# Two-tile groups and a three-stage output in the last layer of a four-layer graph network on one Trainium2 core

## The chip, the cores and the metric

The kernel runs on one core of one Trainium2 chip. The metric is the time of one execution on the device in microseconds (us); of several executions the median counts. TensorE is called PE, VectorE DVE, ScalarE ACT, GpSimd POOL, and SyncE, which here only issues transfers, SP.

## What is computed

Four layers run one after the other on 4096 nodes with 128 features; `adj` is a 4096 x 4096 float32 matrix with few nonzero entries. Each layer adds its result to `x` and normalizes the rows. The change lies in the last layer (L3), and this layer is overlapped with the one before it (L2, attention over the edges):

```python
# L2: attention over the edges of adj (C from per-node scores)
tau = adj_t * jnp.exp(jnp.maximum(0.2 * C, C))
att_weights = tau / jnp.sum(tau, axis=1, keepdims=True)
z = jnp.einsum('mnh,nhf->mhf', adj_t * att_weights, h_prime)
x = _layernorm(x + z.reshape(n, heads * f_out) + bias)
# L3
deg = jnp.clip(jnp.sum(adj, axis=1, keepdims=True), 1.0)
x = _layernorm(x + x @ W_self + (adj @ x / deg) @ W_neigh)
```

## The kernel before

The 4096 rows are 32 tiles of 128 (`NT`), or 8 blocks of 512 (`NB`); `TB` is 4. Layers 0 and 1 are dense products with `adj` and end near 1311 us of the profile. Beside them DVE makes a list of each row's nonzero entries. What follows uses this list (`sparse_layers`, L1405).

**The loop over the tiles** (L1699 to L1724) does layer 2 for tile t, and layer 3 for the tiles before it. The order of PE, DVE, ACT and POOL is the order of the program (L1653); nothing is reordered. In turn:

- POOL issues nine gathers for tile t + 2 (`gathers`, L1491), with a small operation after every second one. The tile `got` has four buffers.
- PE multiplies some *units* of layer 3. A unit is one 128 x 512 float32 product in `layer3_product` (L1597); the profile counts it as two matmuls. `multiply(n)` (L1665) takes n units, and before each one DVE adds finished sums to `acc3` (`add_up`, L1609). With `held=True` nothing is added, and it ends once two sums wait.
- `edges(t)` (L1513) is layer 2's chain for the tile, mostly on DVE: scores, Exp on ACT (L1529), the weighted rows `gw` (L1532), and the sum `here` (L1534). `sums` (L1537) on PE, `divide` (L1544) on DVE and `turn` (L1553), a transpose and the row statistics, follow.
- At the last tile of a *group*, `layer3_rows` (L1560) is put into a queue called `chains`, and three steps of it are taken: a copy on ACT (L1564) with the root for 1/std, the product with W3 on PE (L1573), and the scaling on ACT of `y` (L1577) and `x` (L1583), after which ACT loads Exp's table again (L1584). In the next iteration `begin` (L1673) puts the group's units into the queue `pieces`; so a group's units can start one iteration after its last tile.

The groups are listed in `sizes` (L1696): 1, 1, 2, then six groups of 4, then 2, 1, 1. A group of n tiles has 8 n units; n of them accumulate in one PSUM tile, which DVE then adds to `acc3` in one addition (L1615; the first group is copied by ACT, L1613). The adjacency comes in loads of 1 MB with five buffers (`columns`, L1589), each for 4 / n blocks. The last tile has no units; the output phase takes it in.

Per iteration there are places for 2 + 1 units before `edges`, 4 held ones beside it, 2 held ones after `sums`, and 3 at the end. The last column of `y`, which makes the row sums of `adj`, is set to 1 by a DVE memset after each scaling (L1578). `y` lies in the buffer of `xT`.

**The output phase** (L1729 to L1736) takes the 8 blocks in turn. `layer3_end` (L1617): PE transposes `acc3` back and adds the last tile's share (L1625, L1627); DVE takes 1/deg, and makes the four rows `o` (L1632); ACT squares three of them (L1638), and DVE one (L1640). After the `yield` come the root on ACT (L1643), its reciprocal on DVE (L1644), the scaling on ACT and POOL (L1648, L1650), and SP's store (L1651). The second half of block ib - 1 is issued after the first half of block ib. `o` lies in the tile `rows`, which has room for all 8 blocks.

Of the kernel before, what the change touches and what calls it, by code (L numbers as in the profile page):

```python
# [11 lines left out]
F32 = mybir.dt.float32  # L12
# [4 lines left out]
AF = mybir.ActivationFunctionType  # L17
ALU = mybir.AluOpType
# [3 lines left out]
P = 128  # L22
IB = 512
TB = IB // P
# [19 lines left out]
def adj_resnorm_d4(ctx: ExitStack, tc: tile.TileContext, x_in, xT_in, adj, adjT, w0g, w0gT, a0, w1a, b1a,  # L44
# [7 lines left out]
    nc = tc.nc  # L52
    N, F = x_in.shape
    NT = N // P
    NB = N // IB
# [1349 lines left out]
    def sparse_layers(enter, lists, w, h0T):  # L1405
# [85 lines left out]
        def gathers(t):  # L1491
            if t >= NT:
                return
            got[t] = l2.tile([P, E, F + H], F32, name="got", bufs=4)
            for j in range(E):
                nc.gpsimd.indirect_dma_start(got[t][:, j, :], None, table,  # L1496
                                             bass.IndirectOffsetOnAxis(ap=lists.source[:, t, j:j + 1], axis=0))
                if j % 2:
                    lists.pause()
# [60 lines left out]
        def layer3_rows(t0, n):  # L1560

            s = small.tile([P, n], F32, name="rstd2")
            xb = l2.tile([P, n, P], F32, name="oT")
            nc.scalar.copy(xb, turned.pop(t0))  # L1564
            inverse(s, mv[:, t0:t0 + n, 1])
            yield
            qs = []
            for k0 in range(0, n, 2):
                m = min(2, n - k0)
                q = ps_x.tile([P, m, 2, F], F32, name="px")  # L1570
                qs += [(k0 + k, q[:, k]) for k in range(m)]
                for k in range(m):
                    nc.tensor.matmul(q[:, k].rearrange("p s f -> p (s f)"), xb[:, k0 + k, :],  # L1573
                                     W3.rearrange("p s f -> p (s f)"), start=True, stop=True)
            yield
            for k, q in qs:
                nc.scalar.activation(y[:, t0 + k, :], q[:, 0, :], AF.Copy, scale=s[:, k:k + 1])  # L1577
                nc.vector.memset(y[:, t0 + k, F - 1:F], 1.0)  # L1578
            for k, q in qs:
                if n == 1:  # L1580
                    nc.vector.tensor_scalar_mul(x[:, t0 + k, :], q[:, 1, :], s[:, k:k + 1])
                else:
                    nc.scalar.activation(x[:, t0 + k, :], q[:, 1, :], AF.Copy, scale=s[:, k:k + 1])  # L1583
            nc.scalar.activation(warm, eps, AF.Exp)  # L1584
            yield
# [31 lines left out]
        def layer3_end(t0, n, ib, a):  # L1617


            p = ps_p.tile([P, TB, F], F32, name="pp")  # L1620
            o = rows[:, ib * TB:(ib + 1) * TB, 0:F]
            s = small.tile([P, 2, TB], F32, name="less", bufs=3)
            for k in range(TB):
                at = slice(ib * IB + k * P, ib * IB + (k + 1) * P)
                nc.tensor.matmul(p[:, k, :], acc3[:, at], ident, start=True, stop=False)  # L1625
                for r in range(n):
                    nc.tensor.matmul(p[:, k, :], a[:, r, k * P:(k + 1) * P], y[:, t0 + r, :], start=False, stop=r == n - 1)  # L1627
            r = small.tile([P, TB], F32, name="rdeg")
            nc.vector.tensor_scalar_max(r, p[:, :, F - 1], 1.0)
            nc.vector.reciprocal(r, r)  # L1630
            for k in range(TB):
                nc.vector.scalar_tensor_tensor(o[:, k, 0:F - 1], p[:, k, 0:F - 1], r[:, k:k + 1], x[:, ib * TB + k, 0:F - 1],  # L1632
                                               op0=ALU.mult, op1=ALU.add, accum_out=s[:, 0, k:k + 1])
            nc.vector.tensor_scalar_mul(o[:, :, F - 1], s[:, 0, :], -1.0)
            for k in range(TB):
                junk = l2.tile([P, F], F32, name=f"z{k // 3}")
                if k < 3:
                    nc.scalar.activation(junk, o[:, k, :], AF.Square, accum_out=s[:, 1, k:k + 1])  # L1638
                else:
                    nc.vector.scalar_tensor_tensor(junk, o[:, k, :], 1.0, o[:, k, :], op0=ALU.mult, op1=ALU.mult,  # L1640
                                                   accum_out=s[:, 1, k:k + 1])
            yield
            nc.scalar.activation(s[:, 1, :], s[:, 1, :], AF.Sqrt, bias=eps, scale=1.0 / F)  # L1643
            nc.vector.reciprocal(s[:, 1, :], s[:, 1, :])  # L1644
            for k in range(TB):
                scale = s[:, 1, k:k + 1]
                if k < 2:
                    nc.scalar.activation(o[:, k, :], o[:, k, :], AF.Copy, scale=scale)  # L1648
                else:
                    nc.gpsimd.tensor_scalar(o[:, k, :], o[:, k, :], scale, None, op0=ALU.mult)  # L1650
            nc.sync.dma_start(out[ib * IB:(ib + 1) * IB, :].rearrange("(k p) f -> p k f", p=P), o)  # L1651

        with tc.manual_schedule(engines={mybir.EngineType.PE, mybir.EngineType.DVE, mybir.EngineType.Activation,  # L1653
                                         mybir.EngineType.Pool}):
            chains, pieces = deque(), deque()

            def one(queue, n=1):
                while queue and n:
                    r = next(queue[0], queue)
                    if r is not queue:  # L1660
                        n -= 1
                    else:
                        queue.popleft()

            def multiply(n, held=False):  # L1665
                for _ in range(n):
                    if not held:
                        add_up()
                    elif len(adds) > 1:
                        break  # L1670
                    one(pieces)

            def begin(t0, n):  # L1673
                pieces.append(layer3_product(t0, n))
                return
                yield

            for ib in range(NB):
                p = ps_p.tile([P, IB], F32, name="pp")
                for c in range(NB):  # L1680
                    a = chunk(ld, adjT, ib, c)
                    for k in range(TB):
                        nc.tensor.matmul(p, w[:, c * TB + k, :], a[:, k, :], start=c == 0 and k == 0,  # L1683
                                         stop=c == NB - 1 and k == TB - 1)
                    one(chains)
                end = block_end(ib, p)
                next(end)
                chains.append(end)
            load_spread(0)
            while chains:  # L1690
                one(chains)
            gathers(0)
            gathers(1)
            lists.check()
            targets(0)
            sizes = [1, 1, 2] + [TB] * 6 + [2, 1, 1]  # L1696
            groups = [(sum(sizes[:i]), n) for i, n in enumerate(sizes)]
            of = {t: g for g in groups for t in range(g[0], sum(g))}
            for t in range(NT):  # L1699
                t0, n = of[t]  # L1700
                gathers(t + 2)
                if t % TB == 1:
                    load_spread(t // TB + 1)
                targets(t + 1)
                multiply(2)
                one(chains)
                multiply(1)
                add_up()
                multiply(4, held=True)
                made = edges(t)  # L1710
                add_up()
                if t == t0 + n - 1:
                    nc.scalar.activation(warm, eps, AF.Sqrt)
                so = sums(*made)
                multiply(2, held=True)
                divide(t, so)
                turn(t, t0, n)
                if t == t0 + n - 1:
                    chains.append(layer3_rows(t0, n))
                    if t < NT - 1:  # L1720
                        chains.append(begin(t0, n))
                for _ in range(3):
                    one(chains)
                    multiply(1)  # L1724
            while chains or pieces:
                one(chains)
                multiply(2)
            add_up()
            ends = deque()  # L1729
            late = [columns(NT - 1, 1, ib) for ib in range(0, NB, TB)]  # L1730
            for ib in range(NB):
                ends.append(layer3_end(NT - 1, 1, ib, late[ib // TB][:, ib % TB]))
                next(ends[-1])
                if ib:
                    next(ends.popleft(), None)
            next(ends.popleft(), None)  # L1736

    network(True)
    with tc.If(nc.values_load(flag[0:1, 0:1], min_val=0, max_val=2 * P) != 0):
# [33 lines left out]
```

## Time and profile before

| | us |
|---|---|
| median of 3 runs (1900.08 to 1912.03) | 1908.64 |
| profiled execution, its own time | 1786.93 |
| span of its instructions | 1785.1 |
| first and last gather on POOL start | 1335.57, 1707.81 |
| first matmul of the output phase (L1625) | 1744.59 |
| store instructions of the output phase | 1755.05 to 1775.85 |
| PE, DVE, ACT, POOL busy in the span | 1632.3, 1066.5, 350.9, 435.3 |

All times inside the profile are us from the start of the span. Rows of a timeline give start, duration, engine, line, operation, output and input with their shapes, the count of instructions merged in the row, and in brackets how long the engine was idle before it and what ended this. A group row gives busy time and the mean in ns, then the idle time before the group's instructions. The profiled execution is 6.4% below the median of the runs; the granted clock of TensorE, mean 0.955 over the span, is known for the profiled execution only.

### The profile page before, as it was taken

How to read it: one execution, taken by the hardware profiler on the slowest of the kernel's cores; microseconds unless marked ns; L12 is line 12 of the kernel's file. 1: busy time of each engine (PE TensorE's matmuls, PEld its weight loads, DVE VectorE, ACT ScalarE, POOL GpSimd, SP SyncE). 2: the span in 40 equal slices, each digit the busy share in tenths (PEclk: the TensorE clock that was granted, in tenths of full speed). 3: DMA queues.
4: the chain of work that ended last, by engine and by line, in shares of the span. 5: the costliest groups of instructions: out<-in, count | busy, mean ns of one | idle time of the engine just before them, and what ended most of it. 6: DMA issues, size and time to landing. Idle time of an engine off the chain costs nothing.

```text
span 1785.1 us, 15746 instructions
## 1 busy us (share of the span) xinstructions
PE 1632.3 (91%) x4964; PEld 773.6 (43%) x4968; DVE 1066.5 (60%) x3043; ACT 350.9 (20%) x628; POOL 435.3 (24%) x636
## 2 busy tenths in 40 slices
PE   7999999999999999999999999999965677888794
PEld 3344445544444444444444444444432344444443
DVE  6655447888877876767966421232334655655664
ACT  5865501100000110101000000121222111111123
POOL 0000000000000000000463543000008888888822
PEclk9999999999999999999999999999986788888897
DMA  9987665788888567656878778888874566766682
GB/s 384 373 324 278 247 219 183 247 319 304 294 296 305 212 247 256 249 212 245 291 257 285 273 273 296 300 296 291 296 208 115 195 198 213 238 226 230 219 233 69
DMA packets 89791, 455.04 MB, mean 255 GB/s; under 512 B 15585, under 2 KB 25826, under 8 KB 40674
## 3 DMA queue, kind: packets, MB, share of 16 engines
q1 hardware_dynamic: 68112, 422.93, 66.6%
q0 software_dynamic: 12288, 19.54, 4.6%
q10 hardware_dynamic: 9298, 11.47, 1.9%
q8 instruction: 41, 0.67, 0.1%
q14 instruction: 52, 0.43, 0.1%
HBM read 446.48 MB, written 7.41 MB: 254 GB/s over the span
## 4 chain that ended last, share of the span: by engine, by line
PE 73%; POOL 8%; DVE 8%; DMA 5%; issue 3%; ACT 2%; ACTq 0%; DVEq 0%; SPq 0%; POOLq 0%
PE pacc L687 35%; PE pp L1683 12%; PE pacc L397 11%; POOL got L1496 7%; PE pp L1604 4%; DMA chunk<-in_adjT 2%; DVE here L1534 2%; PE pmm L716 1%; DMA got<-table,source 1%; DVE gw L1532 1%; DMA keep<-in_adjT 1%; PE ptr L397 1%; PE pden L385 1%; PE px L1573 1%; PE ptr L155 1%
## 5 line engine op out<-in xcount | busy, mean ns | idle before, releaser
L1496 POOL DMA_INDIRECT got<-table,source x288 | 276.4, 960 | 307.4 <-issue 304.0
L1386 POOL DMA_INDIRECT value<-in_adjT,where x96 | 99.2, 1034 | 639.3 <-DVE bad L1314 527.2
L1604 PE MATMUL pp<-chunk,xT 128*128 128x512 f32 x496 | 234.6, 619 | 1.3 <-DVE xT L1578 1.0
L687 PE MATMUL pacc<-chunk,v 128*128 128x512 f32 x512 | 225.4, 595 | 0.0
L1683 PE MATMUL pp<-chunk,w 128*128 128x512 f32 x512 | 224.6, 592 | 0.0
L687 PE MATMUL pacc<-chunk,t 128*128 128x512 f32 x512 | 223.5, 592 | 0.0
L687 PE MATMUL pacc<-chunk,x 128*128 128x512 f32 x512 | 222.1, 592 | 0.0
L397 PE MATMUL pacc<-chunk,hw 128*128 128x512 f32 x408 | 186.7, 601 | 0.9 <-DVE hw L439 0.7
L1274 DVE MAX8 top<-chunk 128x8 f32<-128x512 f32 x224 | 144.1, 681 | 59.3 <-DMA chunk<-in_adjT 59.3
L1275 DVE FIND_INDEX8 at<-top,chunk 128x8 uint16<-128x512 f32 x224 | 151.3, 686 | 0.0
L687 PEld LDWEIGHTS pacc<-chunk,v 128*128 128x128 f32 x512 | 95.9, 190 | 117.0 <-issue 117.0
L687 PEld LDWEIGHTS pacc<-chunk,x 128*128 128x128 f32 x512 | 96.2, 190 | 115.8 <-issue 115.8
L687 PEld LDWEIGHTS pacc<-chunk,t 128*128 128x128 f32 x512 | 96.1, 190 | 115.3 <-issue 115.0
L1683 PEld LDWEIGHTS pp<-chunk,w 128*128 128x128 f32 x512 | 95.1, 190 | 109.3 <-issue 108.6
L1604 PEld LDWEIGHTS pp<-chunk,xT 128*128 128x128 f32 x496 | 93.1, 199 | 98.3 <-issue 89.5
L397 PEld LDWEIGHTS pacc<-chunk,hw 128*128 128x128 f32 x408 | 74.1, 190 | 91.0 <-issue 85.9
L328 DVE TENSOR_SCALAR pos<-chunk 128x2048 bf16<-128x2048 f32 x66 | 80.4, 1222 | 44.8 <-DMA chunk<-in_adjT 42.0
L369 ACT ACTIVATE junk<-chunk 128x2048 fp8e4<-128x2048 f32 x51 | 97.4, 1909 | 23.3 <-DMA chunk<-in_adjT 22.6
L1615 DVE TENSOR_TENSOR acc<-pp,acc 128x512 f32<-128x512 f32 x80 | 54.6, 687 | 68.7 <-PE pp L1604 68.5
L1540 PE MATMUL so<-gw,into 128*128 128x132 f32 x192 | 34.5, 325 | 59.4 <-DVE gw L1532 59.4
L1249 POOL IOTA i<- 128x384 int32 (+3 forms) x4 | 1.0, 259 | 331.8 <-PE pden L385 317.7
L1540 PEld LDWEIGHTS so<-gw,into 128*128 128x128 f32 x192 | 29.4, 224 | 76.0 <-issue 42.2
(303 smaller groups left out, 1665.8 us busy)
## 6 DMA issues: line engine op xcount, KB each, us to landing
chunk<-in_adjT SPq DMA_DIRECT2D x386, 1024.0 KB, 4.9
keep<-in_adjT SPq DMA_DIRECT2D x13, 1024.0 KB, 7.8
spread<-spread ACTq DMA_DIRECT2D x16, 384.0 KB, 5.3
got<-table,source POOLq DMA_INDIRECT x288
table<-rows ACTq DMA_DIRECT2D x8, 264.0 KB, 6.5
xT<-in_xT ACTq DMA_DIRECT2D x8, 256.0 KB, 8.0
out<-rows SPq DMA_DIRECT2D x8, 256.0 KB, 2.3
value<-in_adjT,where POOLq DMA_INDIRECT x96
```

Of the source, the lines that this page charges most:

```text
L328: r = nc.vector.tensor_scalar(pos, a, 0.0, None, op0=ALU.is_gt)
L369: nc.scalar.activation(junk, a, AF.Relu, scale=-1.0, accum_out=bad[:, n:n + 1], saturate=False)
L397: in_order(nc.tensor.matmul(p, hw[:, j * TB + k, :], a[:, k, :], start=first and k == 0, stop=last and k == TB - 1))
L687: nc.tensor.matmul(p, stationary(c * TB + k), a[:, k, :], start=n == 0 and k == 0, stop=n == NB - 1 and k == TB - 1)
L1274: nc.vector.max(self.top[:, t, ib, :], row)
L1275: nc.vector.max_index(self.at[:, t, ib, :], self.top[:, t, ib, :], row)
L1386: pin(nc.gpsimd.indirect_dma_start(self.value[:, c * TB + k, j:j + 1], None, flat, bass.IndirectOffsetOnAxis(ap=self.where[:, c * TB + k, ...
L1496: nc.gpsimd.indirect_dma_start(got[t][:, j, :], None, table, bass.IndirectOffsetOnAxis(ap=lists.source[:, t, j:j + 1], axis=0))
L1540: nc.tensor.matmul(so, into[:, j, :], gw[:, j, :], start=j == 0, stop=False)
L1604: nc.tensor.matmul(p, y[:, t0 + k, :], a[:, ib % (TB // n), k, :], start=k == 0, stop=k == n - 1)
L1615: nc.vector.tensor_add(acc3[:, blk], p, acc3[:, blk])
L1683: nc.tensor.matmul(p, w[:, c * TB + k, :], a[:, k, :], start=c == 0 and k == 0, stop=c == NB - 1 and k == TB - 1)
```

## The change

Three edits. The groups of layer 3 become 1, 1, fourteen times 2, 1, 1. The column of ones in `y` is set once, ahead of the loop, and the scaling on ACT writes 127 columns. The output phase's `layer3_end` has three stages: up to DVE's square; ACT's squares and root; reciprocal, scaling and store. Stage three of block ib - 1 is issued between stage one and stage two of block ib. `o` becomes a tile of its own with three buffers.

```diff
             for k, q in qs:
-                nc.scalar.activation(y[:, t0 + k, :], q[:, 0, :], AF.Copy, scale=s[:, k:k + 1])
-                nc.vector.memset(y[:, t0 + k, F - 1:F], 1.0)
+                nc.scalar.activation(y[:, t0 + k, 0:F - 1], q[:, 0, 0:F - 1], AF.Copy, scale=s[:, k:k + 1])
...
-            o = rows[:, ib * TB:(ib + 1) * TB, 0:F]
+            o = l2.tile([P, TB, F], F32, name="o", bufs=3)
...
             nc.vector.tensor_scalar_mul(o[:, :, F - 1], s[:, 0, :], -1.0)
-            for k in range(TB):
-                junk = l2.tile([P, F], F32, name=f"z{k // 3}")
-                if k < 3:
-                    nc.scalar.activation(junk, o[:, k, :], AF.Square, accum_out=s[:, 1, k:k + 1])
-                else:
-                    nc.vector.scalar_tensor_tensor(junk, o[:, k, :], 1.0, o[:, k, :], op0=ALU.mult, op1=ALU.mult,
-                                                   accum_out=s[:, 1, k:k + 1])
+            junk = [l2.tile([P, F], F32, name=f"z{k}") for k in range(2)]
+            nc.vector.scalar_tensor_tensor(junk[1], o[:, 3, :], 1.0, o[:, 3, :], op0=ALU.mult, op1=ALU.mult,
+                                           accum_out=s[:, 1, 3:4])
             yield
+            for k in range(3):
+                nc.scalar.activation(junk[0], o[:, k, :], AF.Square, accum_out=s[:, 1, k:k + 1])
             nc.scalar.activation(s[:, 1, :], s[:, 1, :], AF.Sqrt, bias=eps, scale=1.0 / F)
+            yield
             nc.vector.reciprocal(s[:, 1, :], s[:, 1, :])
...
             gathers(1)
+            nc.vector.memset(y[:, :, F - 1], 1.0)
             lists.check()
             targets(0)
-            sizes = [1, 1, 2] + [TB] * 6 + [2, 1, 1]
+            sizes = [1, 1] + [2] * 14 + [1, 1]
...
-            for ib in range(NB):
-                ends.append(layer3_end(NT - 1, 1, ib, late[ib // TB][:, ib % TB]))
-                next(ends[-1])
+            for ib in range(NB + 1):
+                if ib < NB:
+                    ends.append(layer3_end(NT - 1, 1, ib, late[ib // TB][:, ib % TB]))
+                    next(ends[-1])
                 if ib:
                     next(ends.popleft(), None)
-            next(ends.popleft(), None)
+                if ib < NB:
+                    next(ends[-1])
```

## Prediction

> **What bounds the kernel now.** I read the page first. Its section 5 shows POOL's gathers, 288 of 0.96 us with short gaps:
>
> ```profile
> L1496 POOL DMA_INDIRECT got<-table,source x288 | 276.4, 960 | 307.4 <-issue 304.0
> ```
>
> They start at 1335.57 and 1707.81; POOL's timeline has no gap over 0.31 us between, so a tile takes 372.2 / 287 x 9 = 11.67 us of POOL. Is that the pace of the loop? DVE's timeline has L1526, which reads the gathered rows, at tiles 20, 24, 28 and 31:
>
> ```profile
> 1589.32 0.17 DVE L1526 TENSOR_TENSOR score<-got,near 128x24 f32<-128x24 f32 x1
> 1637.45 0.18 DVE L1526 TENSOR_TENSOR score<-got,near 128x24 f32<-128x24 f32 x1
> 1685.60 0.17 DVE L1526 TENSOR_TENSOR score<-got,near 128x24 f32<-128x24 f32 x1
> 1725.84 0.17 DVE L1526 TENSOR_TENSOR score<-got,near 128x24 f32<-128x24 f32 x1
> ```
>
> Four tiles take 48.14 us, POOL needs 46.7: the loop itself is slower, and falls behind. Tile 31's gathers were issued by 1708.8 and read 17 us later. So the loop's own chain counts.
>
> The early group of tiles 2 and 3 already has the new size, and shows what its chain costs. PE's timeline over tiles 4 and 5, which multiply its 16 units:
>
> ```profile
> 1394.45 2.08 PE L1573 MATMUL px<-W,oT 128*128 128x256 f32 x4 [0.46 <-ACT oT L1564]
> 1396.32 0.28 PE L1511 MATMUL u<-dst,spread 128*128 128x13 bf16 x3
> 1397.11 5.76 PE L1604 MATMUL pp<-chunk,xT 128*128 128x512 f32 x8 [0.52 <-DVE xT L1578]
> 1402.71 0.84 PE L1540 MATMUL so<-gw,into 128*128 128x132 f32 x6
> 1403.38 0.41 PE L1541 MATMUL so<-here,ident 128*128 128x132 f32 x2
> 1403.63 1.88 PE L1604 MATMUL pp<-chunk,xT 128*128 128x512 f32 x4
> 1405.35 0.29 PE L1557 MATMUL px<-ident,x 128*128 128x128 f32 x1
> 1405.47 2.74 PE L1604 MATMUL pp<-chunk,xT 128*128 128x512 f32 x6
> 1408.05 0.22 PE L1511 MATMUL u<-dst,spread 128*128 128x13 bf16 x3
> 1408.12 6.25 PE L1604 MATMUL pp<-chunk,xT 128*128 128x512 f32 x14
> ```
>
> Two matmuls are a unit: 4 + 2 + 3 + 7 = 16, then none are left. And DVE's L1532 of tiles 3, 4, 5:
>
> ```profile
> 1388.51 1.35 DVE L1532 TENSOR_TENSOR gw<-got,u 128x1152 f32<-128x1152 f32 x1
> 1400.03 1.35 DVE L1532 TENSOR_TENSOR gw<-got,u 128x1152 f32<-128x1152 f32 x1
> 1413.46 1.35 DVE L1532 TENSOR_TENSOR gw<-got,u 128x1152 f32<-128x1152 f32 x1
> ```
>
> Group end to next tile 11.52 us; from there to the second tile 13.43 us.
>
> In the output phase (1744.6 to 1775.5) the DVE groups show the wait to be removed, and the line of stores how long one takes to land:
>
> ```profile
> L1644 DVE RECIPROCAL less<-less 128x4 f32<-128x4 f32 x8 | 1.4, 178 | 9.2 <-ACT less L1643 9.2
> DMA to landing us min/median/max: 2.3/2.3/3.9
> ```
>
> [...] a unit is 0.86 us at 1408 and about 1.7 us at 1397, after an idle PE. [...] The trace has the 1.28 us, but the next ACT operation starts 0.01 us later, so I take 1.28. [...]
>
> **Part 1: groups of two.** Bytes, loads (64), matmuls of units stay. DVE gets 17 x 8 - 8 = 128 additions for 80, 48 x 0.69 = 33 us more. Most of it fits into DVE's waits for PE at L1615 (60.1 us). On the path lies this:
>
> - Group end to next tile: divide, transpose, copy, W3, scaling, table load, Exp, with no units left to cover it: 11.52 us, plus what the now two additions ahead of L1547 cost. L1547 started 4.11 us after L1532 at tile 3 (no addition), 4.33 us at tile 5 (two): + 0.22. At tile 5 the transpose already ran at the slow clock (0.48 us), so I take W3 slow too, as at tile 3 (2.08 us). Sum 11.74.
> - Next tile to second tile: as measured, 13.43.
> - A pair: 25.17 us. Two tiles of a group of four take 24.07. A group of four pays the uncovered passage once for four tiles, the new groups twice.
>
> From L1532 of tile 4 (1400.03, unchanged, since the groups before are the same) to that of tile 30 are 13 pairs: 1400.03 + 13 x 25.17 = 1727.24; before, 1714.31. + 12.93.
>
> Tile 30 to 31: before 12.82. By position in the queue, DVE's last addition ahead of `edges(31)` now follows the third unit instead of the second: one unit, + 0.86.
>
> Backlog after tile 31's W3: before, the timeline has 26 matmuls, 13 units (11.32 us). Counting the places (9 units in a first, 7 in a second tile of a pair) tile 30 starts with 16 units, leaves 7, tile 31 begins with 2, gets 8 more, takes 10 by its end; 3 remain, and 2 come after W3: 5. Gain 8 x 0.86 = 6.9.
>
> Start of the output phase: 1744.59 + 12.93 + 0.86 - 6.9 = 1751.5, **+ 6.9**. The lag behind the gathers grows to about 29 us; a `got` buffer would be late only at some 30, so POOL is not held up.
>
> **Part 2: ones.** 31 memsets of 0.06 us go, with waits of 24.9 us for ACT (DVE's waits, 1371 to 1708). I cost this at nothing: after a group end `edges` waits for Exp, which stands behind the table load on ACT (Exp at 1399.30, its scores ready at 1398.33). Were the load not there, the gain would be about 1 us per pair, 14 in all. The new strided memset is not in the trace: between 0.06 (L1578) and 0.7 us (L1615), on a DVE idle for 13.45 us before tile 0.
>
> **Part 3: output.** Before, a block takes 3.23 us between reciprocals, of which DVE waits 0.98 for the root. Moved behind the next block's first half, the reciprocal would find the root done: 3.23 - 0.98 = 2.25 us. The first block gains more: Sqrt's table load (1751.92) now follows the first squares; first reciprocal at 1751.5 instead of 1753.55. Moved with it: scaling, and SP's store, alone in SP's queue. ACT has 3 squares, root, 2 scalings, some 2.2 us per block: it just fits. The last block pays: its squares stand behind the scaling of block 6, + 1.1 us.
>
> The new `o` has three buffers: block ib waits for the store of block ib - 3. Reciprocal to the end of POOL's scaling is 1.47 us (1753.55 to 1755.02), landing 2.3: 3.8; from the first L1632 to the next reciprocal 1.75, with hand-overs 1.85. Two blocks per 5.65 us, so 2.83 each, not 2.25. Reciprocals, in the old time scale: block 0 at 1751.5, then 2, 4, 6 at 1757.2, 1762.9, 1768.55; the last 2.1 later, at 1770.65. Before: 1773.97. **- 3.3**. Without the buffers' limit it would be about - 5.9.
>
> **Sum.** 6.9 - 3.3 = + 3.6 us on the profile's 1786.93. The runs' median is 1.068 times that, of unknown cause; I scale: + 3.9, **1912.5 us**. Some 1% is what a measurement of this kernel can tell from no change.
>
> **Rivals.**
>
> - *W3 runs at the fast clock* after a group end (PE multiplied 7 units just before): 1.03 instead of 2.08 us, a pair 24.12, 13 x 1.05 = 13.7 us less: - 10.1, scaled - 10.8, 1898. Against: the slow transpose at tile 5. Chance 0.14.
> - *The gathers become the bound*: the loop needs no more than POOL, 23.33 us a pair: 13 x 1.84 = 23.9 less, - 20.3, scaled - 21.7, 1887. For: shorter backlogs, no memset waits. Against: tiles 3 to 5. Chance 0.07.
> - *The output doesn't get shorter*: stores land after 3.9 us (the maximum), two blocks per 7.15 us, and block 7 at 1775.3: + 1.3 instead of - 3.3; sum + 8.2, scaled + 8.8, 1917. The change then doesn't do what it says. Chance 0.15.
> - *Slower*: after each group end PE stays slow for longer. At tile 4 it was fast after 7 us from W3's start (1394.45 to about 1401.5), in groups of four after 5.2. [...] + 25.7, scaled + 27.4, 1936. Chance 0.14.
> - The forecast: 0.50, its own range 1906 to 1919.
>
> Range: forecast, third and first rival hold 0.79 and reach from about 1892 to 1922 with the 0.3% by which the runs scatter; I take the upper end to 1932[...]. Faster by over 1% (below 1889.6) is the second rival with the tail of the first, 0.08; slower by over 1% (above 1927.7) most of the fourth, 0.13; within, 0.79.
>
> **What would show it.** L1532 of tiles 4, 6, 8 some 25.2 us apart, W3 at 2.1 us for 4 matmuls, no units between a group end and its W3; L1625 first at 1751; 10 matmuls after tile 31's W3; L1615 128 times; DVE idle ahead of L1632 on a store from block 3 on, blocks 2.8 us apart. Wrong would be a pair near 23.3 or above 26, gathers with gaps, or a wait at L1644.

## The result, and the profile after

The changed kernel takes 1904.05 us (median of 22 runs, 1901.6 to 1906.74), the kernel before 1904.68 us (22 runs, 1888.9 to 1912.28) beside it. The ratio is 1.000, 95% interval 0.9984 to 1.0015. The forecast was 1912.5 us, + 0.2% on the 1908.64 us shown; no difference was measured, and + 0.2% lies just above the interval.

The profiled execution of the kernel after spans 1902.6 us and agrees with its runs. That of the kernel before, 1785.1 us, did not agree with its own. So the two traces differ by 117.5 us where the runs differ by nothing, and no difference between them may be put down to the change before that is cleared up.

Where are the 117.5 us? Up to the first gather both are alike (1335.6 and 1336.7 us). After it, in the groups of the profile after (busy us, mean ns, idle before, what ended most of it):

```profile
L1496 POOL DMA_INDIRECT got<-table,source x288 | 277.5, 964 | 412.3 <-issue 302.8
L1603 PE MATMUL pp<-chunk,xT 128*128 128x512 f32 x496 | 266.7, 681 | 37.7 <-DVE acc L1614 27.3
...
L1614 DVE TENSOR_TENSOR acc<-pp,acc 128x512 f32<-128x512 f32 x128 | 83.5, 684 | 104.5 <-PE pp L1603 59.2
```

The gathers cost what they did (0.96 us each), but POOL now stood idle for 412.3 us instead of 307.4. The additions are 128, as forecast. The units wait for additions (27.3 us), and the additions for units: a circle, so something in it must be late. Two tiles in DVE's timeline, from the L1532 of tile 13, the last of its group, to that of tile 15:

```profile
1590.82 1.35 DVE L1532 TENSOR_TENSOR gw<-got,u 128x1152 f32<-128x1152 f32 x1
...
1601.47 1.35 DVE L1532 TENSOR_TENSOR gw<-got,u 128x1152 f32<-128x1152 f32 x1
...
1613.83 0.69 DVE L1614 TENSOR_TENSOR acc<-pp,acc 128x512 f32<-128x512 f32 x1 [4.29 <-PE pp L1603]
1618.08 1.89 DVE L1614 TENSOR_TENSOR acc<-pp,acc 128x512 f32<-128x512 f32 x3 [3.56 <-PE pp L1603]
...
1621.74 1.35 DVE L1532 TENSOR_TENSOR gw<-got,u 128x1152 f32<-128x1152 f32 x1
```

And PE in the second half of it:

```profile
1609.27 4.44 PE L1603 MATMUL pp<-chunk,xT 128*128 128x512 f32 x6
1613.55 0.22 PE L1511 MATMUL u<-dst,spread 128*128 128x13 bf16 x3
1613.63 2.93 PE L1603 MATMUL pp<-chunk,xT 128*128 128x512 f32 x6
1618.83 3.83 PE L1603 MATMUL pp<-chunk,xT 128*128 128x512 f32 x5 [2.27 <-DVE acc L1614]
```

From group end to the next tile it takes 10.65 us (forecast 11.74), but from there to the second tile 20.27 us (forecast 13.43). In this second part PE's rows say that three units were done by 1613.7 and three more by 1616.6; DVE adds one at 1613.83, and the next only at 1618.08, three in a row. PE in turn has no free PSUM tile until 1618.8. Nothing in the rows occupies DVE between 1614.5 and 1618.1: it waits for a signal of PE.

In the output phase the wait for the root is smaller now (L1642 waits 3.1 us in all, L1644 waited 9.2 before), and a wait for the stores has come. DVE's reciprocals, and the rows' computation where it waits:

```profile
1872.23 0.18 DVE L1642 RECIPROCAL less<-less 128x4 f32<-128x4 f32 x1 [0.58 <-ACT less L1640]
...
1874.65 0.18 DVE L1642 RECIPROCAL less<-less 128x4 f32<-128x4 f32 x1 [0.24 <-ACT less L1640]
...
1876.16 0.35 DVE L1631 SCALAR_TENSOR_TENSOR o<-pp,rdeg,x 128x127 f32<-128x127 f32 x1 [1.06 <-POOL o L1648]
...
1877.79 0.17 DVE L1642 RECIPROCAL less<-less 128x4 f32<-128x4 f32 x1
...
1878.55 0.35 DVE L1631 SCALAR_TENSOR_TENSOR o<-pp,rdeg,x 128x127 f32<-128x127 f32 x1 [0.33 <-DMA out<-o]
...
1880.21 0.18 DVE L1642 RECIPROCAL less<-less 128x4 f32<-128x4 f32 x1
...
1881.68 0.35 DVE L1631 SCALAR_TENSOR_TENSOR o<-pp,rdeg,x 128x127 f32<-128x127 f32 x1 [1.03 <-DMA out<-o]
...
1883.31 0.17 DVE L1642 RECIPROCAL less<-less 128x4 f32<-128x4 f32 x1
```

From block 3 on DVE waits for the store of three blocks ago (the row at 1876.16 names POOL, which had done its scaling before; the two later ones name the store). Two blocks take 5.5 to 5.6 us. From the first matmul of the phase to the end it is 37.1 us, before 40.0 (there the matmul's row starts at 1745.02; the 1744.59 of the table above is its weight load).

### The profile page after: what moved, and what is told of

Its sections match the earlier page's. It is cut to its first block, busy times and chain, and to the rows that moved or that the text cites. A ratio compares the mean times of both kernels' runs of the same rounds, so it can differ in the third digit from the quotient of the medians.

```text
span 1902.6 us, 15801 instructions
## 1 busy us (share of the span) xinstructions
PE 1663.1 (87%) x4964; PEld 773.8 (41%) x4968; DVE 1091.3 (57%) x3066; ACT 372.1 (20%) x664; POOL 436.4 (23%) x636
## 2 busy tenths in 40 slices
DMA packets 95935, 455.04 MB, mean 239 GB/s; under 512 B 15585, under 2 KB 25826, under 8 KB 52962
## 3 DMA queue, kind: packets, MB, share of 16 engines
q1 hardware_dynamic: 74256, 422.93, 63.8%
## 4 chain that ended last, share of the span: by engine, by line
PE 74%; DVE 10%; DMA 5%; issue 4%; another core or an unknown queue 4%; ACT 2%; POOL 1%; DVEq 0%; ACTq 0%; SPq 0%; POOLq 0%
PE pacc L687 33%; PE pp L1681 12%; PE pacc L397 10%; PE pp L1603 8%; DMA chunk<-in_adjT 2%; DVE here L1534 2%; DVE acc L1614 2%; DVE gw L1532 2%; PE pmm L716 1%; PE px L1573 1%; DMA keep<-in_adjT 1%; PE ptr L397 1%; PE ptr L155 1%; PE pden L385 1%
## 5 line engine op out<-in xcount | busy, mean ns | idle before, releaser
L1496 POOL DMA_INDIRECT got<-table,source x288 | 277.5, 964 | 412.3 <-issue 302.8
L1603 PE MATMUL pp<-chunk,xT 128*128 128x512 f32 x496 | 266.7, 681 | 37.7 <-DVE acc L1614 27.3
L1603 PEld LDWEIGHTS pp<-chunk,xT 128*128 128x128 f32 x496 | 101.0, 219 | 154.3 <-issue 99.6
L1614 DVE TENSOR_TENSOR acc<-pp,acc 128x512 f32<-128x512 f32 x128 | 83.5, 684 | 104.5 <-PE pp L1603 59.2
L1557 PE MATMUL px<-ident,x 128*128 128x128 f32 x32 | 11.5, 361 | 75.1 <-issue 35.5
L1529 ACT ACTIVATE score<-score 128x36 f32<-128x36 f32 x32 | 7.4, 231 | 281.0 <-DVE score L1528 281.0
```

What stands on the lines that cost most here:

```text
L1496: nc.gpsimd.indirect_dma_start(got[t][:, j, :], None, table, bass.IndirectOffsetOnAxis(ap=lists.source[:, t, j:j + 1], axis=0))
L1603: nc.tensor.matmul(p, y[:, t0 + k, :], a[:, ib % (TB // n), k, :], start=k == 0, stop=k == n - 1)
L1614: nc.vector.tensor_add(acc3[:, blk], p, acc3[:, blk])
```

## The experiments

All in all eighteen runs, in five sets. The runs of a set are on one chip, and the kernel before runs beside them. Times of a set are compared within it.

### First set: the change in parts (kernel before: 1890.98 us)

**The kernel before, unchanged**, to see a second profile of it.

> The kernel before, unchanged. Theory A (the first profile of it is typical, its 1785.1 us span stands for the runs): a second profile is again near 1785, four tiles of the loop take 48 us, and the 6% between profile and runs stays unexplained. Theory B (the loop over the tiles has waits in the usual run that the first profile did not have; the changed kernel's profile, span 1902.6 against runs of 1904, has them): the second profile is near 1900, the layers up to 1345 us are unchanged, and the loop from the first gather to the last takes about 490 us instead of 372.

Measured: 1889.68 us, ratio 1.000 (0.9983 to 1.0017); profile 1880.0 us. The step from tile 1 to tile 2 is 50.9 us (12.2 in the first profile), the steps at the ends of the groups of four are 16.6 to 21.3 us (13.9), and that from tile 8 to 9 is 29.0 us (12.6). From the first gather to the last it is 436 us; theory B holds, though it had said 490. These waits are in the kernel before too. The first profile showed an execution without them. What are they? The longest, all engines in one timeline, at tile 1:

```profile
1366.68 0.81 PE L1541 MATMUL so<-here,ident 128*128 128x132 f32 x2 [0.86 <-DVE here L1534]
...
1378.85 0.20 POOL L1392 TENSOR_TENSOR idle<-idle 128x1 f32<-128x1 f32 x1
1378.85 0.18 DVE L1547 RECIPROCAL rd<-so 128x4 f32<-128x4 f32 x1 [12.22 <-remote]
...
1379.83 0.45 PE L1557 MATMUL px<-ident,x 128*128 128x128 f32 x1 [9.41 <-DVE x L1549]
...
1384.44 0.38 SPq L1594 DMA_DIRECT2D chunk<-in_adjT  x1
...
1392.15 0.27 ACT L1564 COPY oT<-px 128x128 f32<-128x128 f32 x1 [26.54 <-remote]
```

PE's last matmul into `so` is done at 1367.5 by its row; DVE, which needs only that, starts at 1378.85, 11.4 us later. PE's transpose is done at 1380.3; ACT, which needs only that, starts at 1392.15, 11.9 us later. (The 26.54 us in its row are all of ACT's idle time.) SP's load needs a buffer that PE has read with its fourth unit, whose row ends at 1369.2; the load goes at 1384.44. The same tile in the first profile of before:

```profile
1365.87 0.49 PE L1541 MATMUL so<-here,ident 128*128 128x132 f32 x2 [0.86 <-DVE here L1534]
1366.40 0.18 DVE L1547 RECIPROCAL rd<-so 128x4 f32<-128x4 f32 x1 [0.58 <-PE so L1541]
...
1367.91 0.27 PE L1557 MATMUL px<-ident,x 128*128 128x128 f32 x1
1368.22 0.27 ACT L1564 COPY oT<-px 128x128 f32<-128x128 f32 x1 [3.04 <-PE px L1557]
```

Here DVE and ACT start 0.04 us after the rows' ends, and SP's load 0.03 us after the fourth unit. In other directions nothing is late: in the second profile DVE's result at 1379.68 is taken by PE at 1379.83, DVE's `here` by PE within 0.06 us in 31 of the 32 tiles, and ACT's Exp by DVE after 0.03 us in all of them; the last two hold in the kernel after too. So in this stretch PE's completions reach DVE, ACT and SP 11 to 15 us late, while signals to PE, and from ACT to DVE, are prompt. In the groups after it ACT's copy (L1564) is on time (in the kernel after 0.04 us behind the transpose's row in each of them); there it is DVE that waits (in the kernel after 104.5 us in all at L1614). Whether the matmuls or their signals were late can't be told from the rows. I call both "held" in what follows.

**Groups of two alone** (`sizes` as in the change, all else as before).

> Only the groups of two. Theory A: +6.9 us on the path, scaled +7.4, ratio 1.004. Theory B: the loop waits for something that does not depend on the groups, so 0 within 0.2%; the profile near 1900 with a pair of tiles about 31 us and not 25.2.

Measured: 1904.17 us, ratio 1.0066 (1.0041 to 1.0091): + 12.5 us by the ratio. Theory A said + 7.4; the sign is right, the size nearly double. Of theory B the long pairs came true (30.3 us on average from tile 6 to 28, 30.5 in the kernel after), its "0 within 0.2%" did not.

**The output phase alone** (three stages, `o` with three buffers).

> Only the three-stage output with its three buffers for o. Both theories: the output phase's reciprocals are 2.8 us apart instead of 3.23, in all -3.3 us, scaled -3.5, ratio 0.998. If the buffers bind more (store landing 3.9 us) +1.3 us; if they do not bind -5.9 us.

Measured: 1888.94 us, ratio 0.9988 (0.9968 to 1.0007), a gain too small for the runs' scatter. The trace shows it: first output matmul to the end 38.1 us, and 40.1 in the kernel before, so - 2.0 where - 3.3 was forecast.

**The ones alone** (set once, no memsets).

> Only the column of ones set once. Theory A: 0, as the Exp behind the table load is later anyway. Rival: up to 7 group ends gain 1 us each, -7 us, ratio 0.996.

Measured: 1891.66 us, ratio 1.0009 (0.9994 to 1.0024). Nothing, as forecast.

### Second set: take the gathers away (kernel before: 1893.75 us)

The held stretches all lie where POOL issues gathers. For the kernels before and after, the gathers of the later tiles are left out:

```diff
         def gathers(t):
             if t >= NT:
                 return
-            got[t] = l2.tile([P, E, F + H], F32, name="got", bufs=4)
+            if t >= 4:
+                got[t] = kept[t % 4]
+                return
+            got[t] = kept[t] = l2.tile([P, E, F + H], F32, name="got", bufs=4)
```

> The kernel before, but POOL gathers rows for tiles 0 to 3 only, and the later tiles read those rows again (that part of the computation is left out). Everything else keeps its instructions. Theory A, the gathers in flight hold back the other engines in the usual runs (the loop's steps at a group end are 18 to 23 us there and were 13.9 in the first profile): from tile 4 on four tiles take 48 us or less, group end to next tile about 13.9, and the run is 50 to 80 us shorter, ratio 0.957 to 0.974. The long wait between tiles 1 and 2 (51 us), which lies beside the first gathers, stays. Theory B, the waits come from TensorE, the chunk loads or the engines' own queues: steps stay at 50 to 58 us per four tiles, run within 10 us, ratio 0.995 to 1.0.

> The kernel after with the same part left out: gathers for tiles 0 to 3 only. Theory A: a pair of tiles takes what the prediction's chain said, 11.7 + 13.4 = 25.2 us instead of the 30.4 measured in the kernel after (of which 18.6 to 20.3 lay between the first and the second tile of a pair). Then the chain was right and the gathers made the difference; this kernel is 3 to 8 us slower than the kernel before with few gathers. Theory B: pairs stay near 30 us, with 18 to 20 us from first to second tile.

Measured: 1799.0 us (0.9519, 0.9441 to 0.9597) and 1803.94 us (0.9535, 0.9458 to 0.9613). Theory A holds in both, though the first is 95 us shorter than before where 50 to 80 were expected (some 3 of the 95 are POOL's drain at the very end of the program, 2.2 us instead of 5.5). The rows' transfers and POOL's pauses go with the gathers, so these runs do not tell which of them matters. The kernel before has steps of 13.9, 12.5, 12.6 and 9.0 us in each group of four from tile 7 on, 48.1 us together. The kernel after without its later gathers, DVE's timeline from tile 16, the first of its group, to tile 18:

```profile
1570.62 1.35 DVE L1536 TENSOR_TENSOR gw<-got,u 128x1152 f32<-128x1152 f32 x1
...
1577.97 0.69 DVE L1618 TENSOR_TENSOR acc<-pp,acc 128x512 f32<-128x512 f32 x1 [1.08 <-PE pp L1607]
1579.85 0.69 DVE L1618 TENSOR_TENSOR acc<-pp,acc 128x512 f32<-128x512 f32 x1 [1.19 <-PE pp L1607]
1581.57 0.69 DVE L1618 TENSOR_TENSOR acc<-pp,acc 128x512 f32<-128x512 f32 x1 [1.02 <-PE pp L1607]
...
1584.02 1.35 DVE L1536 TENSOR_TENSOR gw<-got,u 128x1152 f32<-128x1152 f32 x1
...
1595.31 1.35 DVE L1536 TENSOR_TENSOR gw<-got,u 128x1152 f32<-128x1152 f32 x1
```

13.40 us from the first to the second tile, where the prediction's chain had 13.43, and 10.6 to 11.7 us over the group ends (11.29 in the rows). An addition waits 1.0 to 1.2 us for its unit, where it waited 3.6 to 4.3. The chain of instructions is the same; only the gathers are gone.

In both kernels the stretch beside the first 36 gathers stays: 31.8 and 31.5 us from tile 1 to 2.

**A pause behind every gather** in the kernel after, instead of every second (POOL's operation of 0.20 us).

```diff
-                if j % 2:
-                    lists.pause()
+                lists.pause()
```

> The kernel after, with POOL's short pause (0.20 us) behind every gather instead of every second one; nothing is left out. A tile then takes 9 x 1.32 us of POOL or a little more. If an unbroken string of gathers holds back the others and a pause lets them go (one form of theory A), first to second tile falls from 18.6 to 20.3 towards 13.4 us and the run is 20 to 60 us shorter (0.97 to 0.99). If a pause lets nothing go, or the gathers are not the cause (theory B), the steps and the time stay, ratio 0.998 to 1.003.

**The kernel after again**.

> The kernel after, unchanged, for the sum of the parts: groups alone gave 1.0066, output alone 0.9988, ones alone 1.0009, all on one chip. If the parts add up and the chip is like that one: 1.0063, 0.4 to 0.8% slower than before. If the three parts together hide one another's cost, or the kernel before is as slow as in the first comparison: 1.000, as measured first.

Measured: 1876.17 us with the pauses (0.9939, 0.9913 to 0.9965), 1911.03 us without (1.011, 1.0028 to 1.0193): 35 us less for adding work to POOL. The interval of the second, with four runs, takes in the forecast of 1.0063 and leaves out that of 1.000. First to second tile takes 14.1 to 20.0 us, 17 on average, instead of 19.0 to 20.4. The pauses help, but not fully.

### Third set: a set without held signals (kernel before: 1786.70 us)

> The kernel before with POOL's pause of 0.20 us behind every gather instead of every second one. In the kernel after this took 35 us off (1911 to 1876). Theory A, a pause lets TensorE's held signals through whatever the groups are: the steps at a group end fall from 18 to 23 us towards 13.9, the step from tile 1 to 2 from 51 to some 32, run 20 to 40 us shorter than before, ratio 0.98 to 0.99; and it is 5 to 12 us ahead of the kernel after with the same pauses (1876), the price of groups of two. Theory B, the pauses help only the strings of 18 gathers that groups of two make: within 10 us of before.

> The kernel after with the old groups back, a pause behind every gather, and the output rows kept in place (rows) instead of three buffers of their own; ones once and the three-stage output stay. Against the same pauses in the kernel before: the ones nothing, the output phase 5.9 us shorter if the wait for the stores of three blocks ago was what held its blocks at 2.8 us (then they are 2.25 us apart); about 3 us shorter, blocks still 2.8 us apart, if it was ScalarE or another engine.

> The kernel before with five instead of four buffers for gathered rows. POOL's first string of gathers is then 63 long instead of 54 and ends some 12 us later. Theory A, TensorE's signals are held until the string of gathers ends: the step from tile 1 to 2 grows from 51 to about 63 us, and the run is not shorter, 0 to 12 us longer. Theory C, POOL falls behind because its buffers are late, and that is what costs: fewer waits of POOL, run 10 us or more shorter.

> The kernel before with three buffers for gathered rows. The first string is 45 gathers long and ends near 1395 us. Theory A: the step from tile 1 to 2 falls from 51 to about 39 us, later strings are 9 long and let go sooner, run 5 to 30 us shorter than before. Theory C: POOL waits more for its buffers, the gathers become the bound, run 10 us or more longer.

The last two change one number, `bufs=4` of `got`; the second has the old `sizes` in the kernel after and

```diff
-            o = l2.tile([P, TB, F], F32, name="o", bufs=3)
+            o = rows[:, ib * TB:(ib + 1) * TB, 0:F]
```

Here all 35 runs of the kernel before took 1783.19 to 1792.59 us, as the first profile did, with all gathers in. In all four traces of this set DVE has `so` within 0.6 us of the row's end in every tile. So what is held, or not, went with the set of runs, not with a kernel. The chip alone does not decide it: the record gives the same chip number, 8, for this set and for the first and the fifth, where signals are held. The expectations on held signals (first, third and fourth run) were not tested. What the runs do show:

- Pauses with the old groups: 1796.17 us, 1.0056 (1.0039 to 1.0073). Where nothing is held they cost 9.5 us: the last gather starts at 1726.7 instead of 1707.8.
- Old groups, three stages, rows in place: 1790.64 us, 5.5 us below the kernel with the same pauses. First output matmul to the end 34.2 us instead of 40.2: - 6.0. The forecast for an output phase without the buffers' limit was - 5.9, with blocks 2.25 us apart; they are 2.43 apart. The groups of the rows' computation, in the output phase of the kernel after (three buffers) and of this one, show the wait for the stores and its absence:

```profile
L1631 DVE SCALAR_TENSOR_TENSOR o<-pp,rdeg,x 128x127 f32<-128x127 f32 x32 | 9.3, 347 | 4.9 <-DMA out<-o 3.7 <-POOL o L1648 1.1
...
L1630 DVE SCALAR_TENSOR_TENSOR rows<-pp,rdeg,x 128x127 f32<-128x127 f32 x32 | 9.3, 347 | 0.9 <-DVE rdeg L1628 0.4
```

- Five and three buffers: 1787.03 us, 1.0001 (0.999 to 1.0012), and 1786.73 us, 0.9999 (0.9989 to 1.0009). Where nothing is held the number of buffers is worth nothing, so the kernel has no want of gathered rows (theory C falls).

### Fourth set: how long is a signal held? (kernel before: 1897.85 us)

> The kernel after, unchanged, beside the kernel before in this call. If nothing is held back in this call (before near 1787 us): pairs of 25.2 us, output phase 3.3 us shorter, the prediction's sum of + 3.6 us, so about 1790 us, ratio 1.002 (the two kernels with few gathers differed by 4.9). If signals are held (before at 1873 to 1914 us): pairs near 30 us and 1904 to 1911 us, ratio 1.00 to 1.01.

> The kernel after with the old groups back and the output rows kept in place instead of three buffers; the pauses as they were. With pauses behind every gather this output phase was 6.0 us shorter than that of the kernel before and the run 5.5 us. If that carries over: ratio 0.997, about 5.5 us faster than before, output phase (first matmul to the end) 34 us instead of 40. If it does not (the gathers' end and the output phase interact): 1.000.

> The kernel before with five buffers for gathered rows, for a call in which signals are held. Theory A, the hold lasts until the string of gathers ends: the first string is 63 gathers long, the step from tile 1 to 2 grows from 51 to about 63 us. Theory D, the hold lasts a time of its own: the step stays at 51. Where nothing is held: 13 us and ratio 1.000, as measured.

> The kernel before with three buffers for gathered rows, for a call in which signals are held. Theory A: the first string is 45 gathers long, the step from tile 1 to 2 falls from 51 to about 39 us, later strings are 9 long, and the run is 5 to 30 us shorter than before. Theory D: the step stays at 51. Where nothing is held: 13 us and ratio 1.000, as measured.

Measured, in a set with held signals again: kernel after 1905.26 us, 1.0053 (1.0033 to 1.0073). Old groups with the new output, rows in place: 1892.32 us, 0.9965 (0.9942 to 0.9988), - 5.5 us, output phase 34.2 us: the gain stands without the new groups. Five buffers 1900.65 us, 1.0004 (0.998 to 1.0028); three buffers 1892.64 us, 0.9966 (0.9937 to 0.9995), - 5.2 us where theory A said - 5 to - 30.

The first stretch tells how long the hold lasts. More buffers let POOL issue a longer first string of gathers:

| kernel | first string ends | L1532 of tile 2 | tile 1 to 2 |
|---|---|---|---|
| before, gathers for tiles 0 to 3 only | 1382.6 | 1396.2 | 31.8 |
| three buffers | 1395.8 | 1410.1 | 42.8 |
| four (second profile of before) | 1406.2 | 1414.3 | 50.9 |
| five | 1423.3 | 1428.1 | 61.5 |
| four, nothing held (first profile) | 1708.8 | 1374.8 | 12.2 |

In the held sets tile 2 follows the end of the string by 5 to 14 us, wherever that end is: theory A, and not a stretch of fixed length (theory D). It is not one hold, though. In the second profile of before PE's signals got through at 1378.85, 1392.15 and 1402.65, inside the string that ends at 1406.2: several holds follow one another while the gathers run. The last row shows that a string alone does not hold anything.

### Fifth set: the pauses with the old groups, and the kernel after once more (kernel before: 1891.26 us)

> The old groups, ones once, the three-stage output with its rows kept in place, and a pause behind every gather. Where signals are held (kernel before at 1873 to 1914 us) the pauses took 35 us off the kernel after, and this output phase 6 us off: 30 to 45 us shorter than before, ratio 0.976 to 0.984, if the pauses let signals through with the old groups too; 0.997 if they do so only with groups of two. Where nothing is held: 1.0024 as measured.

> The kernel after once more, for the case that nothing is held in this call (kernel before near 1787 us): pairs of 25.2 us, 1790 us, ratio 1.002, by the prediction's sum; 1.000 if the output phase gains what the groups cost. Where signals are held: ratio 1.000 to 1.011, as measured three times.

Measured, held again: 1885.97 us, 0.9977 (0.9956 to 0.9998), which is no more than the output phase gives (0.9965 in the set before). The pauses show no gain with the old groups. Their trace has mostly strings of 27 to 36 gathers where the kernel without pauses has mostly 9 to 18, and one step of 22 to 30 us in four tiles instead of several smaller ones. Longer strings with longer holds fit theory A. Two things do not: tile 2 is through at 1388.7 us, far ahead of the end of the first string (1423.4), and it is tile 3 that comes 5 us behind that end; and the same pauses took 35 us off groups of two, whose strings stayed 18 long. Both stay unexplained.

The kernel after: 1897.26 us, 1.0029 (1.0015 to 1.0043).

## Where the prediction was right and where it failed

The change was compared four times where signals are held: 1.000, 1.011, 1.005, 1.003. In the first comparison it costs nothing; in the three others it costs something, 0.3 to 1.1%. The prediction's + 0.2% lies between them, but not for its reasons. Step by step, with differences after minus before in us; "held" compares, in the first row, the mean of five profiles with groups of two with that of the first set's first, third and fourth run; in the two others four profiles of the kernel after (in the last row with the first and fourth run alone):

| stretch | forecast | gathers left out | held |
|---|---|---|---|
| L1532 of tile 4 to tile 30 | + 12.9 | 321.8 - 309.0 = + 12.8 | 399.1 - 374.4 = + 24.7 |
| tile 30 to output phase | 0.86 - 6.9 = - 6.0 | 25.0 - 30.7 = - 5.7 | - 5.7 |
| output phase to the end | - 3.3 | 34.56 - 36.92 = - 2.4 | 37.3 - 40.3 = - 3.0 |

- **The failed step is the loop's term, with the base that it was read from.** The prediction priced the loop at + 12.93 us from a profile of 1785 us, whose own runs had a median of 1908.64, and bridged the gap of 122 us by a factor of 1.068, "of unknown cause". Of the gap, the second profile of the kernel before shows 95 us: up to 1336 us there is next to nothing of it, in the output phase nothing (40.0 and 40.1 us), and the rest lies beside the gathers. So the loop's term was to be priced with the held signals in it, where it is + 24.7 us, and no factor on the sum gives that. With the fourth set's profile of the old groups (385.1 us) among the others it is + 22.0; the old groups' profiles scatter from 371 to 385 us.
- **What stays open.** The sum in the held sets is then 24.7 - 5.7 - 3.0 = + 16 us, or + 13 with that profile; by the medians it was - 0.6, + 17.3, + 7.4 and + 6.0 us. Part of the difference is that the three profiled executions of the first set's old groups were on average 6 us below the medians of their kernels. But the mended term leads away from the zero of the first comparison. There the kernel before was slow, 1904.68 us against 1890.98 to 1897.85 in the later held sets, while the kernel after was where it is elsewhere (1904.05 against 1897.26 to 1911.03). Why is not known, as no profile shows an execution of the kernel before in that comparison.
- **Part 1, the chain:** with the later gathers left out the difference is right within 0.2 us over 26 tiles. That is luck in part: the forecast had 327.2 and 314.3 us for the stretch, measured were 321.8 and 309.0, both 5 us less, for different reasons. First to second tile was right (13.41 on average). Group end to next tile was 11.34 on average, not 11.74, and this was the first rival's point. The trace of the kernel after shows the granted clock beside it. In the first pair above (tiles 13 and 14) the four W3 matmuls took 1.13 us at a clock of 1.00 (1596.9 to 1597.9), and the step was 10.65 us; after another group end (1750.4 to 1752.3) they took 2.08 us at 0.50, and the step was 11.73. With the later gathers left out the steps lay between 10.6 and 11.7 us as well. No run shows what sets the clock. The kernel before lost waits with its gathers: the steps to tiles 6, 7 and 11 were 9.2, 9.2 and 10.8 us in the first profile and are 7.5, 7.3 and 9.0 here. In the held sets a pair was 30.2 to 30.7 us on average, above the 26 that the prediction named as refuting it.
- **What the prediction did not count:** the loads keep their bytes, but those of the former groups of four come in pieces half as long; their queue has 74256 packets for 422.93 MB where it had 68112 for the same bytes (packets under 8 KB: 52962, before 40674). Beside few gathers this cost nothing that can be seen; whether it matters in the held sets was not tested.
- **The lag behind the gathers** ("a `got` buffer would be late only at some 30, so POOL is not held up"): wrong in the held sets. POOL waited 92.1 us for L1532 between 1440 and 1800 us. The strings that its waits leave are 18 long, one per pair. Where nothing is held this was not tested.
- **Backlog after tile 31's W3:** right; the timeline of after has 10 matmuls in a row there (4.56 us), and tile 30 to 31 is 13.7 us (12.82 + 0.86).
- **Part 2:** right, nothing, with the old groups (0.9994 to 1.0024). The load of Exp's table ahead of Exp (L1584, after L1583) took 1.28 us each of the 12 times before and the 18 times after. With groups of two alone the step from tile 30 to 31 was 14.6 us, with the ones set once 13.7, so there it may be worth 0.9.
- **Part 3:** right in its reason, the buffers' wait: - 2.0 to - 3.0 with three buffers, - 6.0 with the rows in place, against - 3.3 and - 5.9.
- **Rivals.** The gathers were the bound, but not as the rival had it: not by POOL's time, by what they hold: without the later ones the kernel before was 95 us shorter. The slower rival named PE's clock, and its + 25.7 us was its author's estimate; what the groups of two lost beyond the chain's + 12.9 lies in the held stretches.

What is not settled: why PE's completions are held in some sets of runs and not in others; and by what. It is not a matter of DVE and POOL alone, since ACT (11.9 us) and SP's load (15.2 us) came late too. That POOL is part of it is shown by the runs without gathers, by the strings, and by moments such as 1378.85 above, where DVE goes on in the very hundredth of a microsecond in which POOL's pause begins (in the kernel after 1393.54 and 1393.53, in the last set's first kernel 1386.25 and 1386.24).

The traces hold one more sign. They record the updates of the semaphores, by which the engines signal. Of the 801 updates by PE, DVE, ACT and POOL whose instructions end inside a string of gathers of `got`, 420 (52%) are not recorded within 0.15 us of that end in the trace of the kernel after, where signals are held; of 908 in the first profile of the kernel before, where they are not, none is missing. Outside the strings of the kernel after it is 13 of 370. Inside them it is so for each of the four engines, for DVE too (147 of 350), whose signals PE had in time. So the record, at least, is thinned for all of them; what that says of the cause is open.

What the change costs where nothing is held was measured only with gathers left out: + 4.9 us by the medians (1803.94 - 1799.0), against + 3.6 forecast. The kernel after itself did not run in such a set.

Of the complete kernels in held sets the kernel after with a pause behind every gather has the lowest ratio, 0.9939 (0.9913 to 0.9965); with the old groups such pauses cost 9.5 us where nothing is held. Without more pauses it is the old groups with ones set once and the three-stage output with its rows in place: 0.9965 (0.9942 to 0.9988).

## What to carry to other kernels

If a profile's own time does not agree with the median of the runs, look first for the stage that differs: take another profile before scaling anything, and do not price a change from a profile that the runs do not share. Where GpSimd issues long strings of indirect gathers beside a chain that hops between TensorE and other engines, measure once with the gathers left out, which told the chain's own time from what the gathers hold here (95 us of 1893.75). And when a stage is pipelined deeper, give it buffers for the store's round trip (2.3 us from issue to landing in the first profile), or write in place where the memory is free: three buffers took half or more of this output phase's gain.

## What the runs showed of the hardware

Beside strings of gathers, 1.3 us each (up to 51 in a string in the kernel after), TensorE's completions came late in four sets of runs: in the kernel after by up to 25.4 us at VectorE and 12.6 at ScalarE, in the second profile of the kernel before by 15.2 at SyncE. In one other set VectorE had `so` within 0.6 us in every tile; the kernel before was 104 us shorter there (1786.70 against 1890.98 us). In the second profile of the kernel before VectorE's signals to TensorE (0.06 us in 31 of 32 tiles) and ScalarE's to VectorE (0.03 us) were prompt. In the kernel after four matmuls with W3 took 1.13 us at a granted clock of 1.00 and 2.08 us at 0.50. A pause of 0.20 us on GpSimd behind every gather instead of every second took 35 us off one kernel (1911.03 to 1876.17), gave nothing that could be measured in another (a ratio of 0.9977 with them, 0.9965 without), and cost 9.5 us where nothing was held.
